# VectorE in program order through the feed-forward network, and its first unit by seven block products

## The chip, the cores and the metric

The kernel runs on one core of one Trainium2 chip. The metric is the device time of one execution in microseconds (us). Three runs of the kernel before gave 1084.16, 1084.66 and 1086.73 us, so its median is 1084.66 us. Five engines work side by side: TensorE (PE in the profile, with its weight loads as PEld), VectorE (DVE), ScalarE (ACT), GpSimd (POOL) and SyncE (SP), which issues DMAs. Each executes its own list of instructions in the order in which the list was built, and waits on semaphores for the others.

## The reference

A Perceiver block over 8 batches (B) of 128 rows (S) and 512 columns (D):

```python
x = x + cross_attention(layernorm(x), ctx_768)    # 8 heads of 64, 2048 context rows of 384
x = x + self_attention(layernorm(x))              # causal, softmax along axis 1, / sqrt(512)
h   = relu(layernorm(x) @ w1.T + b1)              # 512 -> 2048 hidden units
out = quantize_e4m3(h) @ quantize_e4m3(w2).T + quantize_e5m10(b2)
x = x + quantize_e5m10(out)
```

The layernorms have no weights. Everything is f32 but for the two quantized formats of the feed-forward network.

## The kernel before, in words

**Cross attention (most of the time).** The loop `for b in range(B): for m in range(NK)` treats batch b by four pairs of heads. In each step TensorE makes the scores of one pair (L504) and the attention of the pair before (L559), and between them a projection of keys or values for the next batch. These projections are done by `block_product` (L311): a matrix product in 20 block products with sums of blocks in place of 24. VectorE moves the scores out of PSUM with their maxima (L508), ScalarE makes the exponentials (L528), VectorE turns them in 32x32 squares (L541), and 16 DMAs on SP's queue put the squares in place (L547). `sums_along_rows(b)` (L569) inverts the softmax sums at the end of a batch, writes them to a line in DRAM by four GpSimd DMAs (L581) and spreads that line over the partitions into `rs` by two more (L584). `rs` is read in the next batch by `normalized` (L607). `after_strips` (L519) is a small ScalarE copy that makes ScalarE's queue wait until VectorE has begun the scores of step m.

**The start.** Keys of batch 0 are made plainly by `k_plain` (L380) from the first half of the context, which SP loads in six DMAs of 128x512 (L218). Seven matmuls on the identity (L215) run before that. The weights come in six pieces on ScalarE's queue (L211).

**Self-attention and the turn to the feed-forward network.** The last batches' self-attention (class `SelfAttention`) is interleaved with the loads and preparations of the feed-forward network. `sa1.read(r)` (L804) adds the result to the row block r, and only then is that block final.

**Feed-forward network.** The rows are two groups g of four batches (512 rows). For each group `group_stats` (L884) makes VectorE take statistics of four row blocks (L890, L892) and ScalarE take a square root (L893), `normed_group` (L896) makes VectorE normalize the four blocks (L898, L902), and `turned_rows` (L908) makes TensorE transpose them, 16 transposes by L94, which ScalarE copies out (L95). The first layer's 2048 hidden units are 16 blocks of 128. Group 0's blocks 0 to 3 are made plainly by `hidden` (L1038): four matmuls of 128x512 each. All other blocks are made four at a time by `FourBlocks` (L1079): seven products in place of eight, each of four matmuls with 256 moving columns, in three calls: `begin` (products a and b), `middle` (c, a, b) and `end` (b, c). They need sums of blocks of the weights (`form_w`, L1059: eight VectorE additions of 128x256 for two pairs) and of the rows (`form_x`, L1066: four additions of 128x512). VectorE adds the banks together (`with_bank`, L1097: five per unit), ScalarE applies the Relu (L1103). `quantize_w2` (L1029) casts the second layer's weights to 8 bits in 16 casts (L1034), each after a DMA on SP's queue into one of two buffers. `output` (L1137) is the second layer for one batch: 16 matmuls; `finish` (L1144) adds, converts and sends it out. The last batch is done in two halves of 256 columns.

**What sets the order.** `tc.manual_schedule(engines={...})` keeps an engine's instructions in the order in which the program names them. Without it a planner places them by its own estimate of when each can begin. TensorE is in program order from L99 to the end; ScalarE and VectorE from L202 and L204, VectorE until `first.close()` (L1180), ScalarE until `in_turn.close()` (L1181). So VectorE's instructions that the program names after L1180 (`form_x`, `form_w`, `quantize_w2`, the second group's statistics and normalization, all of `FourBlocks` and `finish`) are placed by the planner, also ahead of L1180 where VectorE would be idle. The planner orders SP's queue throughout. The loop at the end reads:

```python
    work = [FourBlocks(0, d) for d in range(1, 4)] + [FourBlocks(1, d) for d in range(4)]
    work[0].begin()
    for i, unit in enumerate(work):
        if i == 1:
            xfs.append(turned_rows(1, normed_group(1, *group_stats(1)), "xt1"))
            form_x(1, xfs[1])
        unit.middle()
        if i + 1 < len(work):
            work[i + 1].begin()
            unit.end()
        if i > 2:
            ...
```

Of the kernel before, what the change touches and what calls it, by code (L numbers as in the profile page):

```python
# [9 lines left out]
F32 = mybir.dt.float32  # L10
# [10 lines left out]
P = 128  # L21
# [4 lines left out]
def tile_perceiver_block(  # L26
# [21 lines left out]
    nc = tc.nc  # L48
# [36 lines left out]
    def bank(name):  # L85
        return ps_one.tile([P, 512], F32, tag="bank", name=name)
# [88 lines left out]
    def sum_w(halves, out, eng):  # L175
# [22 lines left out]

        eng.tensor_tensor(s(0), b21, s(1), sub)

    in_turn = ctx.enter_context(ExitStack())
    in_turn.enter_context(tc.manual_schedule(engines={mybir.EngineType.Activation}))  # L202
    first = ctx.enter_context(ExitStack())
    first.enter_context(tc.manual_schedule(engines={mybir.EngineType.DVE}))  # L204


    w_in = keep.tile([P, 2, NKC, D], F32, tag="keep", name="w_in")
# [5 lines left out]
    early = bank("early")  # L213
    for _ in range(EARLY):
        nc.tensor.matmul(early[:, :P], ident, ident, start=True, stop=True)  # L215
    for n in range(2):
        for k in range(NKC):
            nc.sync.dma_start(  # L218
                x_both[:, 0, k, 2 * n : 2 * n + 2],
                ctx_t[0, ts(k, P), ts(n, 512)].rearrange("p (i j) -> p i j", i=2),  # L220
            )
# [158 lines left out]
    def k_plain(f2):  # L380


        k_tile(0, f2)
        for n in range(2):
            pss = [bank(f"k_{f2}_{j}_{n}") for j in range(2)]
            for k in range(NKC):
                for j in range(2):
                    nc.tensor.matmul(  # L388
                        pss[j], wk4[:, k, f2, j, :], x_both[:, 0, k, 2 * n : 2 * n + 2],
                        start=(k == 0), stop=(k == NKC - 1),  # L390
                    )
                if (n, k) == (1, 0):
                    yield
            for j in range(2):
                nc.scalar.copy(kts[0, f2][:, j, ts(n, 512)], pss[j])
# [123 lines left out]
    def after_strips(b, m):  # L519


        seen = small.tile([P, 1], F32, tag="seen", name=f"seen_{b}_{m}")
        nc.scalar.copy(seen, mxs[b, m][:, 0, 0:1])
# [45 lines left out]
    def sums_along_rows(b):  # L569

        nc.vector.reciprocal(
            inverse[:, :NH].rearrange("p (i m) -> p i m", i=2),
            sums[b].rearrange("p (m i) -> p i m", i=2),
        )
        turned = small.tile([P, SQ], F32, tag="inverse_t", name=f"inverse_{b}")
        nc.vector.transpose(turned, inverse)  # L578
        line = dram.tile([NH, P], F32, tag=f"sums{b % 2}", name=f"line_s_{b}")
        for a in range(Q):  # L580
            nc.gpsimd.dma_start(line[:, ts(a, SQ)], turned[a * SQ : a * SQ + NH])  # L581
        rs = tmp.tile([P, D], F32, tag="t", name=f"rs_{b}")
        for i in range(2):
            nc.gpsimd.dma_start(  # L584
                rs[ts(i, DH)],
                line[ts(i, NK)].rearrange("m q -> (m q)").partition_broadcast(DH),
            )
        wides[b] = rs

    def inverse_sums(b):  # L590

# [324 lines left out]
    for b in range(B):  # L916
        last = b + 1 == B
        for m in range(NK):
            scores(b, m)

            if m % 2 and not last:
                after_strips(b, m)
            if m == 1 and b > 0 and not last:
                load_u(b - 1)
            if m == 3 and b > 0 and not last:
                nc.scalar.dma_start(xtd[:, :, ts(b - 1, S)], stats[b - 1])
                nc.scalar.dma_start(xr[:, b - 1, :], xs[b - 1])
            if m == 3 and b < B - 2:
                load_x(b)
            unit = None  # L930
            if m > 0:
                attend(b, m - 1)
            elif b > 0:

                attend(b - 1, NK - 1)
            if m == 0:
                unit = v_proj(b, 1)
            elif not last and m == 1:
                unit = v_proj(b + 1, 0)
            elif not last:  # L940
                unit = k_proj(b + 1, m - 2)
            elif m == 1:
                unit = sa0.keys(sa0.rows)
            elif m == 2:
                unit = sa0.weights_and_values(sa0.rows[:3])
            else:

                sa1 = SelfAttention(1, sap, w)
            if b == m == 0:

                keys = k_proj(0, 1, (1,))
                first_of(keys)
                first_of(keys)
                exps(b, m, 0)
                all_of(keys)
            else:
                exps(b, m, 0)
                if unit and not (last and m > 0):
                    first_of(unit)
            if m == 3 and last:  # L960
                bring_rows()
                for r in sa0.rows:
                    sa0.probabilities(r)
                sa1.stats(B - 2)
            exps(b, m, 1)
            if m == 3 and last:
                sa1.scale(B - 2)
            if b == m == 0:
                all_of(both_weights())
            if m == 0 and last:  # L970
                bring_last_rows()
            if m == 1 and b > 0 and not last:
                row_stats(b - 1)
            if m == 2 and b > 0 and not last:
                norm_rows(b - 1)
            strips = turns(b, m)
            if last and m > 0:

                strips([nc.sync, nc.gpsimd], STRIPS)
            else:  # L980
                strips([nc.sync], STRIPS)
            if m == 0 and b > 0:
                ot = normalized(b - 1, wides[b - 1])
            if m == NK - 1:
                if last:
                    inverse_sums(b)
                else:
                    sums_along_rows(b)
            if unit:
                all_of(unit)  # L990
            if m == 1 and b > 0 and not last:
                row_scale(b - 1)
            if m == 3:
                next_half(b + 2, 0)
            if m == 0:
                next_half(b + 1, 1)
                if not last:
                    load_q(b + 1)
                if b > 0:
                    project(b - 1, ot)  # L1000
                if last:
                    sap, w, sa0 = enter_self_attention()
# [23 lines left out]
    w2 = wff.tile([P, NHC, D], E4M3, tag="w2", name="w2")  # L1026
    b2q = wff.tile([P, D], E5M10, tag="b2q", name="b2q")

    def quantize_w2():  # L1029
        nc.vector.tensor_copy(b2q, b2r)  # L1030
        for c in range(NHC):
            w = tp.tile([P, D], F32, tag="w2f", name=f"w2f_{c}", bufs=2)
            nc.sync.dma_start(w, w2_t[ts(c, P), :])
            nc.vector.tensor_copy(w2[:, c, :], w, saturate=False)  # L1034

    hq = wff.tile([P, NHC, B * S], E4M3, tag="hq", name="hq")

    def hidden(g, xt, blocks):  # L1038

        for c in blocks:  # L1040
            ps = bank(f"ph_{g}_{c}")
            for k in range(NK):
                nc.tensor.matmul(  # L1043
                    ps, w1[:, k, ts(c, P)], xt[:, k, :], start=(k == 0), stop=(k == NK - 1)
                )
            nc.scalar.activation(hq[:, c, ts(g, GT)], ps, AF.Relu, bias=b1c[:, c : c + 1], saturate=False)

# [114 lines left out]
        sa1.exps(r)  # L1164
    for r in two:
        sa1.probabilities(r)
    all_of(sa1.keys(sa1.rows[2:]))
    xfs = [turned_rows(0, xf0, "xt0")]
    for r in sa1.rows[2:]:
        sa1.logits(r)  # L1170
        sa1.exps(r)
# [2 lines left out]
    for r in two:  # L1174
        sa1.read(r)

    hidden(0, xfs[0], range(1))
    for r in sa1.rows[2:]:
        sa1.read(r)
    first.close()  # L1180
    in_turn.close()  # L1181


    form_x(0, xfs[0])
    form_w(slice(2, 4))
    hidden(0, xfs[0], range(1, 4))
    form_w(slice(4, 8))
    quantize_w2()
    form_w(slice(0, 2))
    work = [FourBlocks(0, d) for d in range(1, 4)] + [FourBlocks(1, d) for d in range(4)]  # L1190
    work[0].begin()
    for i, unit in enumerate(work):
        if i == 1:
            xfs.append(turned_rows(1, normed_group(1, *group_stats(1)), "xt1"))
            form_x(1, xfs[1])
        unit.middle()
        if i + 1 < len(work):
            work[i + 1].begin()
            unit.end()
        if i > 2:  # L1200

            b = i - 3
            ps = bank(f"pf_{b}")
            output(b, ps, range(NHC))
            finish(b, ps)
# [5 lines left out]
    for b, ps in enumerate(pss, GB):  # L1211
        output(b, ps, range(NHC - 4, NHC))
        finish(b, ps)
    for i in range(2):
        ps = bank(f"pf_{B - 1}_{i}")
        cols = slice(i * D // 2, (i + 1) * D // 2)
        output(B - 1, ps, range(NHC), cols)
        finish(B - 1, ps, cols)

# [46 lines left out]
```

## Time and profile before

| what | value |
|---|---|
| median of three runs | 1084.66 us |
| the profiled execution itself | 1084.88 us |
| its span, first to last instruction | 1083.1 us |
| TensorE matmul busy | 1076.2 us, 99% of the span |
| VectorE busy | 756.5 us, 70% |
| ScalarE busy | 349.0 us, 32% |
| GpSimd busy | 256.5 us, 24% |
| DMA, mean | 126 GB/s |

The span is what the profile shows; the 1.8 us between it and the execution's time lie around it. A group's line in the profile names a line of the kernel, an engine, an operation and its tiles, with the time one instruction took. A wait is idle time of an engine, with the instruction that ended it. An f32 matmul in the source is two matmul instructions in the profile, each with its weight load, so 16 matmuls there are 32 here. The recorded time of a matmul is longer than the distance from one to the next, since they are pipelined; what counts is the distance, which the chain of work shows as the length of a stretch.

### The profile page before, as it was taken

The numbers are of one execution on the slowest core, as the hardware profiler recorded it, in microseconds if no ns is written. First come the engines' busy times: TensorE is split into PE (matmuls) and PEld (weight loads), VectorE is DVE, ScalarE is ACT, GpSimd is POOL, SyncE is SP. The second block draws the span as 40 slices with busy tenths as digits, with TensorE's granted clock in tenths as the row PEclk, the third lists the DMA queues.
The fourth block names the chain that finished last, engine by engine and source line by source line (L and its number), as shares of the span: only waits on it lengthen the run. The fifth ranks groups of instructions, "written<-read, shape, count | busy, mean of one in ns | idle before, by whom it ended". The sixth has DMA issues, their size and how long they took to land.

```text
span 1083.1 us, 15585 instructions
## 1 busy us (share of the span) xinstructions
PE 1076.2 (99%) x5610; PEld 706.6 (65%) x5610; DVE 756.5 (70%) x1639; ACT 349.0 (32%) x552; POOL 256.5 (24%) x393
## 2 busy tenths in 40 slices
PE   9999999999999999999999999999999999999998
PEld 5475784577467647754775578557746656768875
DVE  4876477778777777787788778777877657584333
ACT  3322233324332422432243224332433222323221
POOL 0154130451065015501550162046001312000000
PEclk9999999999999999999999999999999999999999
DMA  9476434553565456545544653455345745431001
GB/s 329 137 186 146 126 78 98 146 147 78 129 165 138 96 131 165 138 90 152 148 110 94 170 146 78 117 146 147 78 112 126 236 120 146 175 105 32 10 17 52
DMA packets 73421, 136.62 MB, mean 126 GB/s; under 512 B 29360, under 2 KB 37568, under 8 KB 72320
## 3 DMA queue, kind: packets, MB, share of 16 engines
q1 hardware_dynamic: 61120, 113.03, 40.3%
q0 software_dynamic: 4880, 12.90, 3.9%
q10 hardware_dynamic: 7344, 9.70, 2.9%
q8 instruction: 45, 0.74, 0.3%
q14 instruction: 32, 0.26, 0.1%
HBM read 55.85 MB, written 10.52 MB: 61 GB/s over the span
## 4 chain that ended last, share of the span: by engine, by line
PE 98%; DMA 1%; ACT 1%; DVE 1%; issue 0%; ACTq 0%; SPq 0%
PE pv_z L428 21%; PE pk_z L405 20%; PE sc L504 10%; PE po L559 10%; PE pv_b L428 4%; PE pk_b L405 3%; PE ph_b L1091 3%; PE psk L739 3%; PE psv L783 3%; PE pf L1139 3%; PE pq L472 3%; PE py L666 3%; PE ph_c L1091 2%; PE ph_a L1091 2%; PE k L388 2%; PE ph L1043 1%
## 5 line engine op out<-in xcount | busy, mean ns | idle before, releaser
L528 ACT ACTIVATE p<-p,nm 128x2048 f32<-128x2048 f32 x64 | 128.2, 2003 | 276.7 <-DVE nm L516 197.1
L541 DVE STREAM_TRANSPOSE p<-p 128x512 f32<-128x512 f32 x256 | 158.8, 679 | 61.9 <-ACT p L528 61.9
L508 DVE TENSOR_SCALAR_CACHE_REDUCE p<-sc 128x512 f32<-128x512 f32 x256 | 159.0, 687 | 23.0 <-PE sc L504 19.4
L428 PE MATMUL pv_z<-wv_sums,x_both 128*128 128x256 f32 x640 | 157.9, 381 | 0.0
L405 PE MATMUL pk_z<-x_both,wk_sums 128*128 128x512 f32 (+1 forms) x320 | 149.2, 572 | 1.0 <-ACT kt L325 0.6
L428 PEld LDWEIGHTS pv_z<-wv_sums,x_both 128*128 128x128 f32 x640 | 120.4, 190 | 18.6 <-issue 2.4
L559 PEld LDWEIGHTS po<-pT,v 128*64 128x64 f32 x2048 | 111.1, 137 | 23.8 <-issue 22.3
L504 PE MATMUL sc<-kt,q 64*128 64x512 f32 x512 | 119.2, 602 | 0.0
L559 PE MATMUL po<-pT,v 128*64 128x128 f32 x2048 | 118.9, 274 | 0.0
L428 PE MATMUL pv_z<-wv_sums,m_both 128*128 128x256 f32 x448 | 107.4, 380 | 0.2 <-ACT v L325 0.2
L405 PEld LDWEIGHTS pk_z<-x_both,wk_sums 128*128 128x128 f32 x320 | 59.2, 190 | 67.2 <-issue 55.0
L405 PE MATMUL pk_z<-m_both,wk_sums 128*128 128x512 f32 (+1 forms) x224 | 101.3, 568 | 0.0
L581 POOL DMA_DIRECT2D line_s<-inverse x28 | 14.6, 526 | 353.3 <-DVE inverse L578 353.3
L428 PEld LDWEIGHTS pv_z<-wv_sums,m_both 128*128 128x128 f32 x448 | 84.1, 190 | 13.2 <-ACT v L325 0.8
L504 PEld LDWEIGHTS sc<-kt,q 64*128 64x128 f32 x512 | 47.4, 186 | 65.8 <-issue 53.9
L165 POOL TENSOR_TENSOR m_both<-x_both 128x256 f32<-128x256 f32 x70 | 51.3, 732 | 157.2 <-DMA x_both<-in_ctx_t_dram 145.9
L325 ACT COPY v<-pv_z 128x512 f32<-128x512 f32 x112 | 62.8, 585 | 55.4 <-PE pv_z L428 55.1
L325 ACT COPY kt<-pk_z 128x512 f32<-128x512 f32 (+1 forms) x112 | 59.8, 563 | 58.3 <-PE pk_z L405 57.9
L405 PEld LDWEIGHTS pk_z<-m_both,wk_sums 128*128 128x128 f32 x224 | 40.8, 190 | 46.8 <-issue 35.1
L165 POOL TENSOR_TENSOR x_both<-x_both 128x256 f32<-128x256 f32 x98 | 70.2, 736 | 0.8 <-DMA x_both<-in_ctx_t_dram 0.8
L328 DVE TENSOR_TENSOR v<-pv_z,v 128x512 f32<-128x512 f32 x96 | 63.1, 685 | 5.5 <-PE pv_z L428 5.5
L328 DVE TENSOR_TENSOR kt<-pk_z,kt 128x512 f32<-128x512 f32 (+1 forms) x96 | 59.9, 651 | 5.8 <-PE pk_z L405 5.4
(213 smaller groups left out, 1263.9 us busy)
## 6 DMA issues: line engine op xcount, KB each, us to landing
pT<-p SPq DMA_DIRECT2D x488, 128.0 KB, 2.4
x_both<-in_ctx_t_dram SPq DMA_DIRECT2D x45, 512.0 KB, 5.3
w<-in_w_t_dram SPq DMA_DIRECT2D x1, 4096.0 KB, 13.9
w2f<-in_w_t_dram SPq DMA_DIRECT2D x16, 256.0 KB, 2.7
pT<-p POOLq DMA_DIRECT2D x24, 128.0 KB, 4.4
x_in<-in_x_dram SPq DMA_DIRECT2D x8, 256.0 KB, 6.7
qd<-xq SPq DMA_DIRECT2D x8, 256.0 KB, 2.5
q<-qd SPq DMA_DIRECT2D x8, 256.0 KB, 4.0
```

The costliest lines, as they stand in the source:

```text
L165: eng.tensor_tensor(x_block(b, h, to), x_block(b, h, one), x_block(b, h, two), ALU.add if op == "+" else ALU.subtract,)
L325: nc.scalar.copy(outs[ij], views(ps))
L328: nc.vector.tensor_tensor(outs[to], views(ps), outs[other], op)
L405: nc.tensor.matmul(ps[:, : n * BK], wk_sums[:, WSLOT[WAT[r]], f2, :], x_block(b, hs, XAT[r]), start=start, stop=True, skip_group_check=True,)
L428: nc.tensor.matmul(ps[:, ts(t, 256)], x[:, ts(t, P)], wv_sums[:, WSLOT[WAT[r]], :], start=start and t == 0, stop=True, skip_group_check=True,)
L472: nc.tensor.matmul(ps, wq[:, k, ts(m, P)], xt[:, k, :], start=(k == 0), stop=(k == NK - 1),)
L504: nc.tensor.matmul(pair[i], q[r, :], kts[b, m // 2][r, m % 2, ts(n, 512)], start=True, stop=True)
L508: nc.vector.tensor_scalar(p[:, :, i].rearrange("p g (t i) -> p t g i", i=SQ)[:, ts(n, Q)], pair[i].rearrange("p (t g i) -> p t g i", g=Q, ...
L528: nc.scalar.activation(p[:, :, i], p[:, :, i], AF.Exp, bias=nms[b, m][:, i : i + 1], scale=SCALE, accum_out=sums[b][:, h : h + 1],)
L541: nc.vector.transpose(p[:, g, i], p[:, g, i])
L559: nc.tensor.matmul(pos[b][h * DH : (h + 1) * DH, ts(m, P)].rearrange("p (a i) -> p a i", a=Q), v[:, jt % 8, ts(2 * m + h, DH)], turned_[b, ...
L1091: nc.tensor.matmul(self.ps[to][:, ts(t, HR)], w[:, q, 2 * self.d + t], x[:, q], start=start and t == q == 0, stop=True, skip_group_check=True,
```

## The change

Five things change.

1. VectorE's region of program order is opened on the exit stack that lives to the end (`ordered`), so it doesn't end before the feed-forward network.
2. `hidden` is gone. Group 0's blocks 0 to 3 become a FourBlocks unit like the others, so there are eight units. Its forms are named earlier (`form_w(slice(0, 2))` and `form_x(0, ...)` ahead of the last logits), the other forms and the casts of w2 are spread over the first units, and the second group's statistics, normalization and transposes are named at i == 2, which is again the unit with d == 2 of group 0.
3. `rs` is loaded by ScalarE's queue in the next batch's step m == 0, after `after_strips`, in place of GpSimd's queue at the end of the batch.
4. The first DMA of the context is split into two of 128x256, and the matmuls that read it likewise.
5. The last batch's output is cut into 384 and 128 columns in place of 256 and 256.

```diff
+    ordered.enter_context(tc.manual_schedule(engines={mybir.EngineType.DVE}))
     in_turn = ctx.enter_context(ExitStack())
     in_turn.enter_context(tc.manual_schedule(engines={mybir.EngineType.Activation}))
-    first = ctx.enter_context(ExitStack())
-    first.enter_context(tc.manual_schedule(engines={mybir.EngineType.DVE}))
...
+    for i in range(2):
+        nc.sync.dma_start(x_both[:, 0, 0, i], ctx_t[0, ts(0, P), ts(i, BK)])
     for n in range(2):
-        for k in range(NKC):
+        for k in range(n == 0, NKC):
...
-                for j in range(2):
-                    nc.tensor.matmul(
-                        pss[j], wk4[:, k, f2, j, :], x_both[:, 0, k, 2 * n : 2 * n + 2],
-                        start=(k == 0), stop=(k == NKC - 1),
-                    )
+                for i in range(2 if f2 == n == k == 0 else 1):
+                    for j in range(2):
+                        to, of = slice(0, 512), slice(2 * n, 2 * n + 2)
+                        if f2 == n == k == 0:
+                            to, of = ts(i, BK), slice(i, i + 1)
+                        nc.tensor.matmul(
+                            pss[j][:, to], wk4[:, k, f2, j, :], x_both[:, 0, k, of],
+                            start=(k == i == 0), stop=(k == NKC - 1), skip_group_check=True,
+                        )
...
-        rs = tmp.tile([P, D], F32, tag="t", name=f"rs_{b}")
+        wides[b] = line
+
+    def spread_sums(b):
+        line = wides[b]
+        rs = wides[b] = tmp.tile([P, D], F32, tag="t", name=f"rs_{b}")
         for i in range(2):
-            nc.gpsimd.dma_start(
+            nc.scalar.dma_start(
                 rs[ts(i, DH)],
                 line[ts(i, NK)].rearrange("m q -> (m q)").partition_broadcast(DH),
             )
-        wides[b] = rs
...
+            if m == 0 and b > 0:
+                after_strips(b, m)
+                spread_sums(b - 1)
...
+    form_w(slice(0, 2))
     all_of(sa1.keys(sa1.rows[2:]))
     xfs = [turned_rows(0, xf0, "xt0")]
+    form_x(0, xfs[0])
     for r in sa1.rows[2:]:
         sa1.logits(r)
         sa1.exps(r)
...
-    hidden(0, xfs[0], range(1))
+    work = [FourBlocks(g, d) for g in range(NG) for d in range(NHC // 4)]
+    work[0].begin()
     for r in sa1.rows[2:]:
         sa1.read(r)
-    first.close()
+    form_w(slice(2, 4))
     in_turn.close()
...
-    form_x(0, xfs[0])
-    form_w(slice(2, 4))
-    hidden(0, xfs[0], range(1, 4))
-    form_w(slice(4, 8))
-    quantize_w2()
-    form_w(slice(0, 2))
-    work = [FourBlocks(0, d) for d in range(1, 4)] + [FourBlocks(1, d) for d in range(4)]
-    work[0].begin()
+    nc.vector.tensor_copy(b2q, b2r)
     for i, unit in enumerate(work):
-        if i == 1:
+        if i == 2:
             xfs.append(turned_rows(1, normed_group(1, *group_stats(1)), "xt1"))
             form_x(1, xfs[1])
         unit.middle()
+        if i < GB:
+            quantize_w2(range(4 * i, 4 * i + 2))
+        if i == 0:
+            form_w(slice(4, 6))
         if i + 1 < len(work):
             work[i + 1].begin()
             unit.end()
-        if i > 2:
-
-            b = i - 3
+        if i < GB:
+            quantize_w2(range(4 * i + 2, 4 * i + 4))
+        if i == 1:
+            form_w(slice(6, 8))
+        if i >= GB:
+
+            b = i - GB
...
-    for i in range(2):
+    for i, cols in enumerate((slice(0, D - P), slice(D - P, D))):
         ps = bank(f"pf_{B - 1}_{i}")
-        cols = slice(i * D // 2, (i + 1) * D // 2)
```

More of the change, by code (lines that the diff above doesn't have):

```diff
@@ L1027, in tile_perceiver_block, with quantize_w2 @@
     b2q = wff.tile([P, D], E5M10, tag="b2q", name="b2q")
-    def quantize_w2():
-        nc.vector.tensor_copy(b2q, b2r)
-        for c in range(NHC):
+    def quantize_w2(blocks):
+        for c in blocks:
             w = tp.tile([P, D], F32, tag="w2f", name=f"w2f_{c}", bufs=2)
@@ L1036, in tile_perceiver_block @@
     hq = wff.tile([P, NHC, B * S], E4M3, tag="hq", name="hq")
[L1038 to L1046, printed above, removed]
     HR = GT // 2
```

## The prediction

> **What bounds the kernel now.** I read the share of busy time, then what TensorE waited for, then the chain of work that ended last, and only then the stretch in which the change lies. From the page and the list of TensorE's waits:
>
> ```profile
> PE 1076.2 (99%) x5610; PEld 706.6 (65%) x5610; DVE 756.5 (70%) x1639; ACT 349.0 (32%) x552; POOL 256.5 (24%) x393
> PE 98%; DMA 1%; ACT 1%; DVE 1%; issue 0%; ACTq 0%; SPq 0%
> PE pk_z L405 <- ACT kt L325: 0.6, 1, 0.6
> PE pk_z L405 <- DVE kt L331: 0.5, 1, 0.5
> PE pv_z L428 <- ACT v L325: 0.2, 1, 0.2
> ```
>
> TensorE is the bound: 1076.2 of 1083.1 us, with 1.3 us of waits after its first instruction. So every column of a matmul that goes is a gain, every wait put before TensorE is a loss, and what other engines save is worth nothing while TensorE doesn't wait for them. The margin to look at is how early its operands are ready. The chain through the change's place (start, length, both in us):
>
> ```profile
> 949.66 3.43 PE ph L1043 x8
> 953.10 1.72 PE pr L806 x4
> 954.81 10.30 PE ph L1043 x24
> ...
> 975.47 3.45 PE ph_b L1091 x16
> 978.92 1.73 PE ph_c L1091 x8
> 980.65 1.75 PE pt_f L94 x16
> ```
>
> TensorE goes from the last product of a unit (ph_c, L1091) to the second group's transposes (pt_f, L94) without a gap. Why there is none stands in the timeline:
>
> ```profile
> 952.93 1.88 PE L806 MATMUL pr<-sv,e 128*128 128x512 f32 x4
> ...
> 960.14 0.69 DVE L890 BATCH_NORM_STATS2 fst<-rows 128x6 f32<-128x512 f32 x1
> ...
> 961.07 1.87 DVE L890 BATCH_NORM_STATS2 fst<-rows 128x6 f32<-128x512 f32 x3
> ...
> 968.10 1.00 DVE L902 TENSOR_SCALAR xn_f<-rows,fmv,frs 128x512 f32<-128x512 f32 x2
> ...
> 980.49 1.91 PE L94 MATMUL pt_f<-ident,xn_f 128*128 128x128 f32 x16
> ```
>
> The last reads of self-attention end at about 955; the planner lets VectorE take the second group's statistics at 960 and end the normalization at 969, eleven us before TensorE wants it. The program names these steps later, after the additions of the unit before.
>
> What program order means is shown one group earlier, where VectorE is already held to it:
>
> ```profile
> 916.38 0.36 DVE L892 BATCH_NORM_AGGREGATE fmv<-fst 128x2 f32<-128x6 f32 x4
> 921.69 0.69 DVE L609 TENSOR_TENSOR rs<-po,rs 128x512 f32<-128x512 f32 x1 [4.95 <-ACT rs L604]
> 922.30 0.17 DVE L898 RECIPROCAL frs<-fsd 128x4 f32<-128x4 f32 x1
> ```
>
> The square root was there at 917.5, yet the reciprocal (L898) stood behind L609, which waited 4.95 us. Nothing overtakes.
>
> **The first unit by seven products.** Gone: 16 matmuls of 512 columns, 3.43 + 10.30 = 13.73 us of the chain. New: seven products; 16 matmul records, two products, take 3.45 us, so 7 x 1.726 = 12.08. Gain **1.65 us**, all on the path. VectorE gets five additions more (0.69 each), ScalarE one copy; both have room (VectorE is busy 17.3 of 25 us from 955 to 980).
>
> **VectorE in order, second group.** At i == 2 TensorE's next instructions are the transposes. VectorE reaches the statistics only behind unit 1's last addition, and that needs unit 1's last product, which is what TensorE does directly before the transposes. So from that product's end TensorE waits for all of this in turn (distances between starts from the rows above and their neighbours): 0.20 until the addition begins (as from 1006.41 to 1006.61 in a later unit), 0.61 for it, two casts 0.68, eight additions of `form_w(6:8)` 2.69 (from 942.60 to 945.29), four statistics 2.38, aggregates 0.37, square root with its two hand-overs 0.44 (its table load of 1.28 fits under the additions), reciprocal 0.20, the first normalization 0.55, hand-over 0.10. Sum 8.2 us; the other three blocks come every 0.46 against 0.43 for a row's transposes, +0.1. **8.3 us** on the path, where before there was nothing. Bounds: 7.5 if the hand-overs cost nothing and casts overlap, 9 if each costs 0.1 more.
>
> **The clock after that wait.** Here I look for what a hole on TensorE costs beyond its length. The windows view (stretch, length, ..., granted clock, DMA share, GB/s) and the first matmuls:
>
> ```profile
> 1079.15:1082.40 3.25, 0.00 (x0) 0.00 (x0) 0.85 (x2) 0.00 (x0) 0.00 (x0) 1.00 0.32 112
> 1082.40:1083.10 0.70, 0.00 (x0) 0.00 (x0) 0.00 (x0) 0.00 (x0) 0.00 (x0) 0.55 0.04 12
> L215 PE MATMUL early<-ident x14: 421/421/582, 1.5 to 4.5; 128*128 128x128 f32 x14
> L94 PE MATMUL pt_f<-ident,xn_f x32: 272/273/273, 944.2 to 982.1; 128*128 128x128 f32 x32
> ```
>
> About 3.3 us after the last matmul the clock has fallen to half, so it falls inside a hole of 8.3. At the start the same matmul takes 421 ns in place of 273; weight loads of L388 take 337 ns until 6.87 and 190 from 7.50 on. So the first 5.7 us from 1.53 ran at half speed. Half of 5.7, 2.85 us, is lost if the start repeats. If a rise takes as long as the fall, 3.3, it is 1.65. Bounds 0 and 2.85; I take the middle of 1.65 and 2.85, **2.25 us**, since both rows are of this clock. The Trainium skill, "TensorE: Matmul & The Clock Gate", section "Part 1: The HAM clock gate", speaks against the change too: half clock after an idle window of about 3.4 us, full clock after a busy window as long, windows running free. By the page alone, an estimate, the loss would be 1.7 us when the restart meets a window's start and up to twice that, and the end result 1093.0 to 1094.7.
>
> **VectorE in order, first group.** `form_w(0:2)` begins when w has landed (942.6, as now) and ends at 945.3. `form_x(0)` now stands ahead of the logits of rows 6 and 7; its tile has the tag "sk" of keys that these logits read, so it begins when TensorE has made them, about 947.9, and ends near 950.5. Behind it wait two logits, exponentials and probabilities: ready at about 952.4 and 953.1. TensorE, with unit 0's products a and b in front (949.5 to 952.95), reads them at 952.95 and 953.8. No wait, with some 0.6 us to spare; the cover is those two products. If it fails, 0 to 3 us. After that VectorE has about 10 us of work per 12 us of unit: the forms of unit 1 are done at 959 and wanted at 961. Casts wait for w2f on SP's queue: a buffer is free from the casts half a unit earlier, some 6 us, and a load lands in 2.7. Nothing for it.
>
> **`rs` on ScalarE's queue.** Per batch ScalarE gets a copy (0.19) and two DMA issues (0.33 to 0.45 each), ahead of the exponentials, and GpSimd loses two issues of 0.55. At 314.40 ScalarE had stood idle 14.36 us when the exponentials could begin, and the maxima that release the copy begin at 308.76, so the issues end near 310.5. The line has landed long before (2.1 us). `rs` takes 3.5 us to land on today's queue, so it is there at 314, and `normalized` reads it at 321.4: seven us of cover. GpSimd's next sums wait for the context's DMA at 309.65 anyway. Zero.
>
> **First load and last output.** TensorE's first real matmul waited for the weights (w_in, landed 4.96), not for the context; half a context block earlier helps nothing, and one more issue of 0.4 on SP's queue delays loads that are read microseconds later: -0.1 to +0.3, taken as 0. At the end the last piece has 128 columns: VectorE's two steps fall from 0.42 to about 0.29 each, but 16 matmuls of 128 columns take between 16 x 0.054 (half of today's 256) and 16 x 0.107 (no faster than today), where the weight load of 98 ns may set the pace. TensorE ends between the same time and 0.85 later, VectorE has its piece of 384 to do until then: -0.1 to +0.6, taken as 0, between its ends but nearer the lower since loads of 140 ns at L94 follow each other every 0.107. The same page, section "Back-to-back issue gap", gives about 81 ns for such pairs; by it the estimate is +0.15.
>
> **Sum.** -1.65 + 8.3 + 2.25 = **+8.9 us**. The profiled execution took 1084.88, 0.22 above the median, so 1093.8 for it and **1093.6** beside the median.
>
> **Rivals.**
> - *The order doesn't bind* (the change doesn't do what it says): the statistics slip ahead of the unit's additions, as now. They need 8 us of VectorE under 24 us of TensorE's work. Against it: the 4.95 us at L609. Time 1084.66 - 1.65 = 1083.0: not slower. It decides for "no change" once the wait with its clock is under 4.9 us.
> - *The wait without the clock*: the gate holds. Against it: the 0.55 above. 1084.66 - 1.65 + 8.3 = 1091.3.
> - *A second wait* at the first group: exponentials or PSUM banks come late behind `form_x`. Spare 0.6 us; costs 1 to 3 us: 1094.6 to 1096.6.
>
> **How the numbers follow.** Forecast 0.68, second wait 0.13, no clock loss 0.10, order not binding 0.09. The bounds of the forecast's own terms (wait 7.5 to 9, clock 0 to 2.85, end +0.6) give 1090.5 to 1095.5; with the second wait the range is 1090.7 to 1096.5. It leaves out the case of 1083. Faster or slower counts from 0.3%, about what a measurement of this kernel tells from no change: 3.25 us. Slower 0.90, same 0.08, faster 0.02, since nothing in the change is worth 3.25 us.
>
> **What would show it.** A TensorE wait of 8 us at L94 on VectorE's normalization, with `form_w` and the statistics directly before; a granted clock under 1 in that window; seven products from about 949.5 with no wait at the reads of rows 6 and 7; ScalarE's waits unchanged at the batches' starts. Statistics found before unit 1's last addition would make it wrong.

## The result and the profile after

The kernel after takes 1091.41 us (median of 4 runs, 1091.0 to 1091.87). The kernel before, run beside it, takes 1085.11 us (4 runs, 1084.16 to 1086.73). The ratio is 1.0053 with a 95% interval of 1.0039 to 1.0066, so the change costs 6.3 us and is slower by the 0.3% that count here. The profiled execution took 1091.51 us with a span of 1089.6, against 1084.88 and 1083.1 before.

From the page: the span, the busy times, and the share of each engine in the chain that ended last.

```profile
span 1089.6 us, 15677 instructions
...
PE 1075.1 (99%) x5638; PEld 712.5 (65%) x5638; DVE 760.9 (70%) x1652; ACT 352.1 (32%) x564; POOL 249.1 (23%) x379
...
PE 96%; DVE 1%; DMA 1%; SPq 1%; ACT 0%; issue 0%; ACTq 0%
```

TensorE is busy 1.1 us less than before, while the span is 6.5 us longer: the loss is a wait, not work. Its share of the chain falls from 98% to 96%, and the list of TensorE's waits (us in total, times, longest) names one new item of any size:

```profile
PE pt_f L94 <- DVE xn_f L911: 8.3, 1, 8.3
PE early L214 <- POOL ident masks.py:199: 1.5, 1, 1.5
PE pk_z L411 <- ACT kt L327: 0.6, 1, 0.6
PE k L394 <- DMA x_both<-in_ctx_t_dram: 0.3, 1, 0.3
```

The timeline of the kernel after shows what stands in that wait (start, length, engine, line, out<-in; in brackets the idle time before and its releaser):

```profile
977.65 0.69 DVE L1098 TENSOR_TENSOR u<-ph_c,u 128x512 f32<-128x512 f32 x1 [1.03 <-PE ph_c L1092]
978.26 0.75 DVE L1045 CAST w<-w2f 128x512 fp8e4<-128x512 f32 x2
...
981.85 2.46 DVE L899 BATCH_NORM_STATS2 fst<-rows 128x6 f32<-128x512 f32 x4
...
984.63 0.30 ACT L902 ACTIVATE fsd<-fmv,eps 128x4 f32<-128x4 f32 x1 [4.05 <-DVE fmv L901]
...
985.18 1.91 DVE L911 TENSOR_SCALAR xn_f<-rows,fmv,frs 128x512 f32<-128x512 f32 x4
...
985.87 3.56 PE L94 MATMUL pt_f<-ident,xn_f 128*128 128x128 f32 x16 [8.26 <-DVE xn_f L911]
```

VectorE waits for unit 1's last product, adds it, casts, adds the weights' forms from 979.0 to 981.9, and only then takes the statistics that it took at 960 in the kernel before. The transposes, 1.91 us before, take 3.56. The windows view says why (stretch, length, busy time of PE, PEld, DVE, ACT and POOL, granted clock, DMA share, GB/s):

```profile
977.50:982.38 4.88, 0.11 (x1) 0.00 (x0) 4.66 (x12) 2.25 (x4) 0.00 (x0) 1.00 0.35 107
982.38:985.87 3.49, 0.00 (x1) 0.03 (x1) 3.09 (x11) 0.30 (x1) 0.00 (x0) 0.50 0.00 0
985.87:989.20 3.33, 3.33 (x16) 3.33 (x17) 1.22 (x3) 1.67 (x3) 0.00 (x0) 0.50 0.00 0
989.20:1000.00 10.80, 10.80 (x52) 9.53 (x51) 5.51 (x10) 2.88 (x7) 0.00 (x0) 1.00 0.16 50
```

The clock falls to half at 982.38, 4.8 us into the hole, and comes back at 989.20, 3.33 us after TensorE's restart. Half of 3.33 is 1.67 us lost. (At the very start this column reads 1.00, because a trace's record of the clock begins with the first rise; that TensorE ran at half speed until then shows in the weight loads that the prediction quotes, 337 and then 190 ns.)

At the first group nothing waits: the reads of rows 4 and 5 (L815) are issued at 946.38 and those of rows 6 and 7 at 951.56, without idle time, as `form_x` found its room. VectorE ends the probabilities of row 6 at 950.97 and of row 7 at 951.55, and TensorE reads them at 951.56 and 952.42, so some 0.6 us were to spare, as predicted:

```profile
946.66 0.69 DVE L1074 TENSOR_TENSOR x_forms<-xf 128x512 f32<-128x512 f32 x1 [2.31 <-PE pl L763]
...
951.26 0.29 DVE L786 TENSOR_SCALAR e<-e,sr 128x128 f32<-128x128 f32 x1
...
951.56 1.88 PE L815 MATMUL pr<-sv,e 128*128 128x512 f32 x4
```

One thing doesn't fit the prediction: the kernel after is already ahead before the feed-forward network begins. TensorE's scores of the second batch start 0.35 us earlier than before, later matmuls are 1.04 ahead at 229 us, 1.55 at 538 and 1.40 at 936. The experiments had to explain the wait's price and this lead.

### The profile page after: what moved, and what is told of

The parts are those of the page before. It is cut to its first block, busy times and chain, and to the rows that moved or that the text cites. A ratio compares the mean times of both kernels' runs of the same rounds, so it can differ in the third digit from the quotient of the medians.

```text
span 1089.6 us, 15677 instructions
## 1 busy us (share of the span) xinstructions
PE 1075.1 (99%) x5638; PEld 712.5 (65%) x5638; DVE 760.9 (70%) x1652; ACT 352.1 (32%) x564; POOL 249.1 (23%) x379
## 4 chain that ended last, share of the span: by engine, by line
PE 96%; DVE 1%; DMA 1%; SPq 1%; ACT 0%; issue 0%; ACTq 0%
PE pv_z L434 21%; PE pk_z L411 20%; PE po L565 11%; PE sc L510 10%; PE ph_b L1092 4%; PE pv_b L434 4%; PE pk_b L411 3%; PE psk L748 3%; PE psv L792 3%; PE ph_c L1092 3%; PE ph_a L1092 3%; PE pq L478 3%; PE py L675 3%; PE pf L1140 2%; PE k L394 2%; PE pw L294 1%
## 5 line engine op out<-in xcount | busy, mean ns | idle before, releaser
L529 ACT COPY seen<-mx 128x1 f32<-128x1 f32 x21 | 4.0, 191 | 209.8 <-DVE p L514 209.8
```

## The experiments

Theory: the loss is VectorE's program order at i == 2 (wait 8.3) with the clock behind it (about 1.7), the unit gains 1.65, and something in cross attention gains about 1. Rivals: program order costs by itself wherever it holds; the clock isn't lost, or is lost by the wait's length; the lead is the first load, the tail or chance. Each time is a median; the ratio is to the kernel before on the same chip, with its 95% interval. Edits are to the kernel after unless said otherwise. The runs were taken on three chips, on which the kernel before took 1085.58, 1085.3 and 1084.68; the kernel after was measured apart from them, beside 1085.11. Differences of some tenths between kernels of different chips are therefore not to be trusted.

**The statistics one unit earlier.** Only the place in the program changes.

```diff
     for i, unit in enumerate(work):
+        if i == 1:
+            xf1 = normed_group(1, *group_stats(1))
         if i == 2:
-            xfs.append(turned_rows(1, normed_group(1, *group_stats(1)), "xt1"))
+            xfs.append(turned_rows(1, xf1, "xt1"))
```

> The changed kernel with one move: the second group's statistics and normalization are named at i == 1, one unit before the transposes, VectorE still in program order. Theory (the price is the 8.3 us hole before the transposes and the half clock behind it, 1.65 us): no wait at L94, time 1091.4 - 8.3 - 1.6 = 1081.5, below the kernel before. Rival (program order itself costs, the wait only moves to another place, for instance to the addition of unit 1's middle that now comes 1.5 us later): 1084 to 1090, with a new wait of TensorE's of some us.

Measured: 1081.55 us (5 runs), ratio 0.9965 [0.9951, 0.9979]. The chain through the place (start, length):

```profile
976.00 1.73 PE ph_c L1092 x8
977.73 1.75 PE pt_f L94 x16
979.48 1.73 PE ph_c L1092 x8
```

The wait is gone, and so is the clock's loss: 9.9 us in all. VectorE is in program order here just as in the kernel after; so the order costs nothing by itself, the place of these few lines costs 9.9 us. Run again on another chip:

> The kernel with the statistics named early once more, on the same chip as the one with the first unit made plainly: 1081.5, no wait at L94.

1081.49 us (7 runs), 0.9971 [0.996, 0.9981]: faster than both kernels, with an interval wholly below 1.

**VectorE back to the planner**, with all else as in the kernel after.

```diff
-    ordered.enter_context(tc.manual_schedule(engines={mybir.EngineType.DVE}))
...
+    first = ctx.enter_context(ExitStack())
+    first.enter_context(tc.manual_schedule(engines={mybir.EngineType.DVE}))
...
     form_w(slice(2, 4))
+    first.close()
```

> The changed kernel with VectorE's region of program order closed where the kernel before closes it, so that the planner places the feed-forward network's VectorE work. Theory (nothing but the place of the statistics in VectorE's order costs time): the planner takes them early, no wait at L94, 1081.5 as with the statistics named early. Rival (the eighth unit and the spread forms have a price of their own, or the planner's order brings waits of its own): 1083 to 1088.

Measured: 1082.03 us (6 runs), 0.9968 [0.9957, 0.998]. The planner finds as good a place as the hand did, within 0.5 us. Both undo the same wait in different ways. Most of the 0.5 may be a wait that only this run has, at the reads of rows 6 and 7 (`PE pr L816 <- DVE e L787: 0.6`): the planner put casts and forms ahead of the probabilities. It is the second wait that the prediction had among its rivals, here in another kernel.

**Program order alone**, put into the kernel before without any of the moved names.

```diff
+    ordered.enter_context(tc.manual_schedule(engines={mybir.EngineType.DVE}))
-    first = ctx.enter_context(ExitStack())
-    first.enter_context(tc.manual_schedule(engines={mybir.EngineType.DVE}))
...
-    first.close()
```

> The kernel before with one part of the change: VectorE in program order to the end, nothing named elsewhere. Theory (in program order each wait is the sum of what is named in front): all 16 casts, each pair behind a DMA of w2f, now stand before the first FourBlocks unit's first addition, so TensorE waits at that unit's second use of bank b for about 19 us, then once more some 5 us for the second group's normalization, with half clock behind each: about 27 us in all, 1112. Rival (order by itself costs little, since VectorE is only 70% busy): 1086 to 1092.

Measured: 1115.96 us (2 runs), 1.029 [1.0271, 1.0309]. TensorE's waits:

```profile
PE ph_b L1090 <- DVE u L1096: 21.3, 1, 21.3
PE pt_f L94 <- DVE xn_f L901: 4.6, 1, 4.6
```

In the kernel before all 16 casts are named in one call, and each needs a load first. The timeline of this run shows VectorE waiting for the loads one by one, with the first unit's addition behind them:

```profile
986.38 0.43 DVE L1033 CAST w<-w2f 128x512 fp8e4<-128x512 f32 x1 [1.01 <-DMA w2f<-in_w_t_dram]
988.16 0.43 DVE L1033 CAST w<-w2f 128x512 fp8e4<-128x512 f32 x1 [1.35 <-DMA w2f<-in_w_t_dram]
989.60 0.43 DVE L1033 CAST w<-w2f 128x512 fp8e4<-128x512 f32 x1 [1.01 <-DMA w2f<-in_w_t_dram]
...
992.87 0.68 DVE L1096 TENSOR_TENSOR u<-ph_b,ha 128x512 f32<-128x512 f32 x1
```

The two waits make 25.9 of the 31.0 us by which the span grows. The clock makes most of the rest; the windows from each restart of TensorE on:

```profile
993.61:999.41 5.80, 5.80 (x14) 4.64 (x15) 1.38 (x2) 0.53 (x2) 0.00 (x0) 0.50 0.00 0
1009.92:1013.06 3.14, 3.14 (x15) 3.14 (x16) 1.31 (x3) 1.45 (x3) 0.00 (x0) 0.50 0.00 0
```

Half of 5.80 and of 3.14 is 4.5 us, together 30.4. The expectation was 4 us short: its waits were 24 in place of 25.9, and it allowed some 3 us for the clock in place of 4.5, as the first restart alone cost 2.9. That the change's own wait is only 8.3 fits its spreading of the casts and forms over the units.

**The hole filled with idle matmuls.** TensorE gets 36 matmuls on the identity, whose results nobody reads, in front of the transposes. The wait stays as long; only TensorE's clock is kept up.

```diff
         if i == 2:
+            idle = bank("idle")
+            for _ in range(36):
+                nc.tensor.matmul(idle[:, :P], ident, ident, start=True, stop=True)
```

> The changed kernel with 36 matmuls of 128x128 on the identity put before the second group's transposes, 36 x 0.214 = 7.7 us of work for nothing inside the hole, so that TensorE isn't idle. Theory (the hole's idle time drops the clock, and that costs 1.65 us beyond the wait): granted clock 1.00 throughout the stretch, transposes in 1.9 us in place of 3.56, time 1091.4 - 1.65 = 1089.8. Rival (the clock is no part of the loss): 1091.4.

Measured: 1089.99 us (5 runs), 1.0045 [1.0032, 1.0058]. The windows of this run, with the clock in the third column from the right:

```profile
977.50:985.50 8.00, 7.84 (x71) 7.65 (x69) 7.53 (x22) 2.49 (x4) 0.00 (x0) 1.00 0.22 68
985.50:987.60 2.10, 2.04 (x17) 1.95 (x18) 1.29 (x3) 1.37 (x3) 0.00 (x0) 1.00 0.00 0
```

With the clock at 1.00 throughout, the time is 1.4 us lower by the medians (one of the five runs took 1091.65). The spans are clearer: 1087.3 to 1088.3 in these runs, 1089.1 to 1090.0 in the kernel after, 1.8 apart in the profiled ones. That is the clock's price, apart from the wait's.

**Holes of other lengths.** First, unit 1's last casts and `form_w(6:8)` go behind the normalization, which shortens the wait by their 3.5 us:

```diff
-        if i < GB:
+        if i < GB and i != 1:
             quantize_w2(range(4 * i + 2, 4 * i + 4))
-        if i == 1:
-            form_w(slice(6, 8))
...
             form_x(1, xfs[1])
+            quantize_w2(range(6, 8))
+            form_w(slice(6, 8))
```

> The changed kernel with the two casts and the eight additions of the last forms moved from before the statistics to behind the second group's row forms. Theory (the wait is the plain sum of VectorE's instructions in front of the first normalized block): the wait falls by 0.68 + 2.69 to 4.9 us; with the clock's loss as before 1088.0, without it 1086.4. Rival (something else ends the wait, such as ScalarE's square root with its table load): the wait stays above 7 us and the time at 1091.

Measured: 1088.36 us (10 runs), 1.0026 [1.0017, 1.0035]. The wait is 4.7 us, and in the profiled execution the transposes take 3.52 us, as in the kernel after:

```profile
982.02:985.43 3.41, 3.41 (x17) 3.41 (x17) 1.08 (x3) 1.76 (x3) 0.00 (x0) 0.50 0.00 0
```

In this execution a hole of 4.7 us loses as much clock as one of 8.3. But the price isn't fixed. Three of the ten runs, the profiled one among them, took 1087.18 to 1087.56 at a mean clock of 0.998, the other seven 1088.25 to 1088.86 at 0.996 or 0.997. Another 3.41 us at half speed would lower the mean by 0.0016, so those seven probably had two such stretches, which no trace shows. By the medians the hole cost 2.1 us beyond its length (1088.36 - 1081.55 - 4.7).

Second, the statistics go to i == 1 as well, so that only the reciprocal and the normalization are left in the hole:

```diff
+        if i == 1:
+            scales1 = group_stats(1)
         if i == 2:
-            xfs.append(turned_rows(1, normed_group(1, *group_stats(1)), "xt1"))
+            xfs.append(turned_rows(1, normed_group(1, *scales1), "xt1"))
```

> The statistics named at i == 1, the casts and the last forms behind the row forms, but the reciprocal and the normalization left at i == 2 before the transposes. Theory (the wait is the sum of what stands in front of the first normalized block, and the clock falls only in a hole longer than about 3.3 us): a wait at L94 of 0.20 + 0.61 + 0.20 + 0.55 + 0.10 = 1.7 us, clock 1.00 throughout, 1.7 above the kernel with all of it early: 1083.2. Rival (any hole drops the clock): a stretch at half clock as in the changed kernel, 1084.9.

Measured: 1083.0 us (11 runs), 0.9982 [0.9973, 0.999]. The list of waits says `PE pt_f L94 <- DVE xn_f L911: 1.5`, and the windows of this run:

```profile
977.50:979.30 1.80, 0.26 (x2) 0.09 (x2) 1.53 (x4) 0.98 (x3) 0.00 (x0) 1.00 0.00 0
979.30:985.00 5.70, 5.70 (x35) 5.12 (x36) 4.14 (x9) 2.39 (x6) 0.00 (x0) 1.00 0.01 3
```

A hole of 1.5 us costs 1.5 us (1083.0 against 1081.5 without it, on other chips) and the clock holds. In program order alone the clock fell in a hole of 4.6. Where between 1.5 and 4.6 us that begins, no run here shows.

**The first unit made plainly**, in the version with the early statistics: `hidden` takes the place of unit 0.

```diff
-    work[0].begin()
+    hidden(0, xfs[0], range(1))
...
-        unit.middle()
+        if i == 0:
+            hidden(0, xfs[0], range(1, 4))
+        else:
+            unit.middle()
...
-            unit.end()
+            if i > 0:
+                unit.end()
```

> The changed kernel with the statistics named early, and group 0's blocks 0 to 3 made plainly again by 16 matmuls of 512 columns in place of seven products. Theory (the unit is worth its columns): TensorE's stretch 13.73 us in place of 12.08, 1.65 us above the kernel with the statistics early of the same chip. Rival (the shorter stretch was given back by a wait at the reads of rows 6 and 7 or by VectorE's five additions): less than 0.8 us apart.

Measured: 1083.07 us (11 runs), 0.9985 [0.9976, 0.9993]; on the same chip the version with seven products took 1081.49. The unit gains 1.58 us.

**The kernel before with `rs` on ScalarE's queue**, nothing else of the change.

```diff
-        rs = tmp.tile([P, D], F32, tag="t", name=f"rs_{b}")
+        wides[b] = line
+
+    def spread_sums(b):
+        line = wides[b]
+        rs = wides[b] = tmp.tile([P, D], F32, tag="t", name=f"rs_{b}")
         for i in range(2):
-            nc.gpsimd.dma_start(
+            nc.scalar.dma_start(
...
+            if m == 0 and b > 0:
+                after_strips(b, m)
+                spread_sums(b - 1)
```

> The kernel before with one part of the change: rs loaded by ScalarE's queue in the next batch. Theory (GpSimd's two loads of rs share the DMA engines with the last strips of pT, which holds back VectorE's first score at a batch's start and, in two of seven batches of the profiled execution, TensorE by 0.5 to 0.66 us): no TensorE stall at the scores of batches 1 and 4, 1.2 us less than the kernel before, 1084.4 where that takes 1085.6. Rival (the two stalls are chance and the move is worth nothing, as the prediction had it): 1085.6.

Measured: 1083.02 us (11 runs, 1082.59 to 1083.9), 0.998 [0.9972, 0.9989]: a gain of 2.3 us, more than either theory gave. The scatter of the runs falls too: the kernel before beside it lay between 1082.9 and 1087.64. The start of the second batch shows where it comes from, first in the kernel before, then in this run:

```profile
198.17 1.09 POOL L584 DMA_DIRECT2D rs<-line_s  x2 [2.06 <-DMA line_s<-inverse]
...
203.64 4.36 PE L504 MATMUL sc<-kt,q 64*128 64x512 f32 x16
...
206.13 0.69 DVE L508 TENSOR_SCALAR_CACHE_REDUCE p<-sc 128x512 f32<-128x512 f32 x1 [1.69 <-DMA pT<-p]
```

```profile
202.93 3.70 PE L504 MATMUL sc<-kt,q 64*128 64x512 f32 x16
...
204.09 0.69 DVE L508 TENSOR_SCALAR_CACHE_REDUCE p<-sc 128x512 f32<-128x512 f32 x1 [0.36 <-PE sc L504]
...
205.06 1.14 ACTq L588 DMA_DIRECT2D rs<-line_s  x2
```

In the kernel before GpSimd issues the two loads of `rs` at 198.17, while the last 16 strips of `pT` are on their way. VectorE can't put new scores into `p` until those strips have been read out of it, so its first step waits 1.69 us for a DMA, and TensorE, whose PSUM banks it would have emptied, takes 4.36 us for scores that take 3.70 here. The view of the DMAs between 190 and 207 us (median us from issue to landing, last column) has the strips slower in the kernel before, first, than in this run, second:

```profile
pT<-p SPq DMA_DIRECT2D x16, 128.0 KB, 3.5
```

```profile
pT<-p SPq DMA_DIRECT2D x16, 128.0 KB, 2.4
```

With the loads behind VectorE's first scores (205.06), the strips no longer share the DMA engines with them. At the six later batches the median of the 16 is 2.3 or 2.4 in both kernels, as only the strips behind the loads are late. At the third batch's start these are the last five; again the kernel before (302.5 to 307), then this run (301.1 to 305.6):

```profile
pT<-p SPq DMA_DIRECT2D x5, 128.0 KB, 3.9
```

```profile
pT<-p SPq DMA_DIRECT2D x5, 128.0 KB, 2.3
```

VectorE began 1.68 us after TensorE's scores there, in place of 1.16, and TensorE lost nothing: in the fourteen traces delays of up to 1.7 us cost at most 0.14 us. Where TensorE lost more than 0.2 us, VectorE began 1.8 to 3.5 us after the scores.

**The reverse**: the version with the early statistics, with `rs` back on GpSimd's queue.

```diff
-            nc.scalar.dma_start(
+            nc.gpsimd.dma_start(
...
-            if m == 0 and b > 0:
-                after_strips(b, m)
-                spread_sums(b - 1)
```

> The changed kernel with the statistics named early (1081.55) and rs loaded by GpSimd at the end of the batch again. Theory (the move of rs is worth the stalls at the batches' starts): 1.2 us more, 1082.7, with waits of VectorE on pT's DMA at the first score of a batch. Rival: 1081.5.

Measured: 1083.44 us (12 runs), 0.9987 [0.9978, 0.9996], 1.9 us above the version that it came from; that ran on other chips, and by the ratios to the kernel before the step is 1.7 to 2.4 us. The wait is back, here at a later batch:

```profile
715.00 1.08 POOL L590 DMA_DIRECT2D rs<-line_s  x2 [4.59 <-PE pk_z L411]
...
721.32 0.69 DVE L514 TENSOR_SCALAR_CACHE_REDUCE p<-sc 128x512 f32<-128x512 f32 x1 [2.57 <-DMA pT<-p]
...
722.07 1.12 PE L510 MATMUL sc<-kt,q 64*128 64x512 f32 x2 [0.42 <-DVE p L514]
```

So both ways round the move is worth about 2 us. The starts of TensorE's first scores of batches 1 and 7 (counted from 0), read from the timeline of eight kernels, show all of it. Between them lie six batches of the same matmuls:

| kernel | `rs` loaded by | batch 1 | batch 7 | between |
|---|---|---|---|---|
| before | GpSimd | 203.64 | 821.34 | 617.70 |
| before, split first load | GpSimd | 203.24 | 822.17 | 618.93 |
| before, tail of 384 and 128 | GpSimd | 203.12 | 823.03 | 619.91 |
| early statistics, `rs` back | GpSimd | 203.50 | 822.51 | 619.01 |
| before, `rs` moved | ScalarE | 202.93 | 819.45 | 616.52 |
| after | ScalarE | 203.29 | 819.95 | 616.66 |
| early statistics | ScalarE | 203.16 | 819.68 | 616.52 |
| early statistics, again | ScalarE | 203.02 | 819.53 | 616.51 |

With `rs` on ScalarE's queue a batch takes 102.75 us and next to nothing is lost (at most 0.16 us, once in the kernel after); on GpSimd's, the same stretch loses 1.2 to 3.4 us, differently in each run. The traces of the other six runs agree: 616.50 to 616.65 in the five with ScalarE, 618.55 in program order alone, with GpSimd. In the kernel before it is 0.69 in the first of the six and 0.51 in the fourth. This is the scatter of its runs, too. That the strips wait for the DMA engines, and not for something else that GpSimd's issues do, is the reading that fits the landing times; a load of another size in the same place wasn't tried. Nor was GpSimd kept for a later load, so the moved time and the other queue aren't told apart.

**The split first load alone**, in the kernel before.

```diff
+    for i in range(2):
+        nc.sync.dma_start(x_both[:, 0, 0, i], ctx_t[0, ts(0, P), ts(i, BK)])
...
-        for k in range(NKC):
+        for k in range(n == 0, NKC):
```

> The kernel before with one part of the change: the first context load in two halves, and its matmuls likewise. Theory (TensorE's first matmul waits for the weights, and what it gains depends on when the clock rises, which varies from run to run): within 0.5 us of the kernel before. Rival (half a load lets TensorE start earlier): 0.3 to 1 us less.

Measured: 1084.83 us (11 runs), 1.0001 [0.9992, 1.001]. Nothing.

**The tail of 384 and 128 columns alone**, in the kernel before.

```diff
-    for i in range(2):
+    for i, cols in enumerate((slice(0, D - P), slice(D - P, D))):
-        cols = slice(i * D // 2, (i + 1) * D // 2)
```

> The kernel before with one part of the change: the last batch's output in 384 and 128 columns. Theory (the last DMA of 64 KB ends 0.4 us sooner after VectorE than that of 128 KB, and the last matmuls take 56 ns each): the span's end 2.6 us after VectorE's last instruction in place of 3.05, 0.5 us less in all. Rival (as predicted, nothing): end 3.0 us after it, the time of the kernel before.

Measured: 1085.46 us (11 runs), 0.9998 [0.9989, 1.0007]. My expectation of a gain fell; the rival, nothing, held, as far as an interval of 1 us on either side lets one see. In the traces VectorE ends 0.10 us earlier with the new tail. The last output then lands 2.52 to 2.94 us after VectorE's end in the ten traces with the new tail (2.94 in this run), and 2.65 to 3.05 in the four with the old one: that scatter hides whatever the smaller piece gains.

## Why the prediction was right, and where it wasn't

Forecast: +8.9 us. Measured: +6.3. The direction and the mechanism of the loss were right, and the time lies in the range; one step was wrong and one mis-sized. (The range, 1090.7 to 1096.5, isn't the sum of its bounds, which with a second wait of up to 3 us would be 1090.5 to 1098.5; the time lies in both.)

| term | predicted | measured | by |
|---|---|---|---|
| first unit by seven products | -1.65 | -1.58 | made plainly again |
| wait at the second group | +8.3 | +8.26 | the wait in the trace |
| clock after it | +2.25 | +1.65 | transposes 3.56 for 1.91; filled hole 1.4 to 1.8 |
| second wait, first group | 0 | 0 | no idle time at L815 |
| `rs` on ScalarE's queue | 0 | about -2 | alone -2.3, taken back +1.9 |
| first load | 0 | 0 | alone +0.15, interval holds 0 |
| tail | 0 | 0 | alone, interval holds 0 |
| sum | +8.9 | +6.3 | 1091.41 - 1085.11 |

The row of `rs` differs from run to run. For the two profiled executions alone the spans' 6.5 us are the lead of 1.40 and the unit's 1.65 gained, the wait of 8.26 and 1.8 for the slower transposes lost, and 0.47 gained behind the last product, most of it the last output's landing.

*The wait* came out to 0.04 us because each row of its sum was an instruction that the trace of before already showed, in the order in which the program names them; the links of the chain after are the predicted ones (casts 0.67, forms from 979.01 to 981.94, statistics 2.38, normalization 0.56).

*The clock* was lost as said, in the profiled execution by 1.65 and not 2.25: TensorE was at half speed for 3.33 us after its restart, the lower of the two estimates. That it was the lower one is luck of the moment. In each trace the clock changes only at points that lie multiples of 3.41 us apart; here 985.79 was such a point, and TensorE restarted 0.08 us behind it. In program order alone the restart at 993.61 came 1.03 us behind one, and the clock rose not at the next point (996.00) but at the one after (999.41), 5.80 us later, so that 2.9 us were lost. I took the middle of the two estimates because the program's start looked slower (5.7 us at half speed); but over the runs that rise came anywhere from 5.81 to 7.59 us, so one start was no measure of it. The Trainium skill, "TensorE: Matmul & The Clock Gate", section "Part 1: The HAM clock gate", has windows of about 3.4 us that run free of the work; the runs agree, the changes in a run lie whole multiples of 3.41 us apart, and where they lie differs from run to run.

*The first group* had its room as predicted, some 0.6 us; all of it lay 1.4 us earlier by the lead.

***`rs` on ScalarE's queue* is the step that failed: "`rs` takes 3.5 us to land on today's queue, so it is there at 314, and `normalized` reads it at 321.4: seven us of cover. ... Zero."** It looked at when `rs` is needed and by whom, and at what its new queue does meanwhile. It didn't look at what the loads do on their old place: 256 KB beside strips that the next batch's first instruction waits for. The wait stood in the trace of before, 1.69 us on `DMA pT<-p` at 206.13, and the row of the maxima at 308.76, which the prediction uses, has one of 0.88. I passed over it because VectorE's waits cost nothing while TensorE doesn't wait, and the list of TensorE's waits had no item for it. The 0.66 us at 203.64 lie inside a group of 16 scores that began on time and ended late. Even so the trace of before held only 1.2 us of it; the other traces with `rs` on GpSimd's queue lost 2.0 to 3.4.

*The tail*: matmuls of 128 columns on 8-bit data follow each other every 56 ns, 16 in 0.90 us, so the lower bound of 0.054 was the right one and TensorE did not end later. VectorE's last steps came down to 0.28 and 0.29. No time that can be measured came of it. The same page of the skill, section "Back-to-back issue gap", gives about 81 ns for such pairs in a stream and about 56 for a matmul by itself; the stream here went at the second figure.

*The rivals*: the order does bind, and the clock is lost; the second wait didn't come. That the time is 0.1 from the rival without a clock loss (1091.3) is chance, a loss of 1.65 and an unforeseen gain of about 2 beside it.

The lead of 1.40 us at 936 is then accounted for: 1.04 between batches 1 and 7 (617.70 - 616.66), and 0.35 up to batch 1 (203.64 - 203.29). Most of the second part stands with the clock at the start, which came to full speed at 6.17 us in the profiled execution of after and at 7.27 in that of before: 1.1 us at half speed are 0.55, less the new wait of 0.3 at L394. That part differs from run to run and is no gain of the change.

## What to carry to other kernels

When an engine is put into program order, each group of instructions needs a place in the text as early as its operands exist; walk along the bound engine, and at each read ask what the text names ahead of its producer. A hole on TensorE can cost more than its length: in the traces here holes of 4.6 to 8.3 us cost 1.6 to 1.7 us on top, one of 21.3 us 2.9, by where the restart fell between the points at which the clock can change, and one of 1.5 us nothing. And when a DMA is moved, price its old place too: what else was on the DMA engines then, who waited for that, and whether the bound engine's groups there last longer than their like elsewhere, since the list of waits shows a stall inside a group only in part: nothing of the 0.66 us here, 0.4 of 1.8 us in the reverse run.

## What the runs showed of the hardware

- TensorE's clock keeps a rhythm of its own. In the kernel after it changed at 6.17, 982.38, 989.20 and 1088.19 us; in the kernel before at 7.27 and 1082.47. The distances are multiples of 3.413 us (286, 2 and 29 of them; 315 before). The phase differs from run to run: the first rise came at 5.81 us in one run and at 7.59 in another. After a restart close to one of these points the clock was back at the next (3.14, 3.33 and 3.41 us at half speed), after one 1.03 us behind a point only at the second (5.80 us).
- Matmuls with 8-bit data follow each other every 56 ns at 128 columns, although each weight load is recorded at 98 ns.
- Beside two loads of 128 KB on another queue the last strips of a batch (128 KB each) landed in 3 to 4 us in place of 2.3 to 2.4. Moving the loads by some 7 us, to ScalarE's queue, also took most of the scatter out of the time: from 4.7 us between the lowest and highest of 35 runs to 1.3 in 11.
